# Closing the last expert blocks in order of opening, and combining the last 13 token tiles in three groups

## The chip, the core and the metric

The kernel runs on one core of one Trainium2 chip. The metric is the device time of one execution in microseconds (us). A core has five engines that work side by side and meet at semaphores: TensorE (PE, matrix products; its weight loads are listed as PEld), VectorE (DVE), ScalarE (ACT), GpSimd (POOL) and SyncE (SP). Each takes its instructions in the order of the program, and so does each queue of DMA issues: SP's queue issues the plain transfers here, POOL's the indirect ones (gathers and scatters by a list of row numbers).

## What is computed

The reference is one layer of a graph network on 6250 nodes of 256 features, followed by a mixture of experts. Cut to what matters:

```python
xn = _layernorm(x)
x = x + gnn(xn, edges) + linear_attention(xn)        # 100000 edges
# the experts, on y = _layernorm(x)
gate_logits = y @ gate_w + gate_b                    # 16 experts
topk_vals, topk_idx = jax.lax.top_k(gate_logits, 2)
topk_w = jax.nn.softmax(topk_vals, axis=-1)
h = jax.nn.relu(jnp.einsum('bsh,ehf->bsef', y, w1) + b1)
expert_out = jnp.einsum('bsef,efh->bseh', h, w2) + b2
moe = sum of topk_w * expert_out over the two chosen experts
x = x + _layernorm(y + moe) * gamma + beta
```

## The kernel before

A tile is 128 tokens; there are 49 (`NT`), the last with 106 rows. The kernel works tile by tile through the graph part and the attention. Behind them, when enough tiles have their gate logits, a **phase** (`PHASES`, line 120: tiles 0 to 7, 8 to 11, and so on up to 46 to 48) routes its tiles' tokens to experts. Tokens of one expert are packed into **blocks** of 128 slots, in a buffer in device memory (`w_xslots`). At any time an expert has one open block, which is part full. The phases fill it further, and a full one goes to the end of a queue of blocks to be computed.

- `route` (L771) takes the two best experts of each token, counts, gives each token its slots (`slot_i`), and keeps the state: `s["open"]` is the number of each expert's open block, `s["had"]` whether it has one, `s["queue"]` how many blocks are queued, `s["next"]` the next unused block number, `s["code"]` one number for each place of the queue, which says where the place's block lies and which expert it needs. A small product with the identity (L892) turns `code` into a row, and `listed` (L757) makes the row numbers that SP reads into registers (L968).
- `scatter` (L913) writes the phase's tokens into their slots, by indirect DMAs on POOL (L931).
- `expert` (L964) computes one block j of the queue: SP loads the expert's weights in two pieces (512 KB and 642 KB) and the block's tokens (128 KB), PE transposes (L997) and does both layers (L1007, L1017), ACT the activation (L1013), DVE adds the bias (L1021), and SP stores the block to `w_yslots`. Places for weights: four of each piece.
- `combine` (L1035) finishes two tiles: for each, two gathers from `w_yslots` on POOL (L1047), the normalised token on ACT (L1055), on DVE two weighted additions (L1062), statistics (L315, L316), a normalisation with gamma and beta and the residual (L1070, L1071, L1073), and a store to `out` on SP. There are 14 places for gathered rows.

The number of blocks is fixed at 114 (`USUAL`, L123); places that no tokens fill are computed on a spare row. The phases list 7, 8, ... blocks each; phase 8 lists blocks 63 to 80, phase 9 blocks 81 to 87. The last phase (`flush`) closes all: every expert's open block counts as done, and blocks 88 to 113 are listed in the order of the experts' numbers, an expert's part-full block right behind its full ones.

The order of the work is written by hand. `Weave` (L153) holds pieces of work, each a generator, with the slot at which it goes on; in each slot the pieces that are due issue their instructions, so that every engine's order follows from the slots. Of the later slots: the last phase is routed at 815, block 88 begins at 829 and each next one 4 slots later (block 113 at 929), and a block's store counts as issued 24 slots after its beginning. `combine` of tiles 0 and 1 begins at slot 835, of each next pair 5 slots later. Tiles 36 to 48 are the exception: line 1173 holds them until `block + 24`, slot 953, behind the last block's store.

What a gather waits for is declared by hand too. Every gather would wait for all stores to `w_yslots` issued ahead of it. Phase 8 queues the open blocks that it did not fill as they are (`part`, L818 to L828), so that all tokens of tiles 0 to 35 (`CUT`) lie in blocks 0 to 84 (`FIRST` is 85): their gathers wait for the store of block 84 alone, and not for later ones (L1030 and L1050). The gathers of tiles 36 to 48 wait for all stores.

`usual` (L295) is a flag that the routing multiplies by each of its conditions, such as L894 in the last phase: the queue must be at most 114 blocks long. If one fails, a second pass (L1220 on) computes all 128 possible blocks and combines all tiles again.

Of the kernel before, what the change touches and what calls it, by code (L numbers as in the profile page):

```python
# [23 lines left out]
F32 = mybir.dt.float32  # L24
# [215 lines left out]
def windowed_layer(ctx: ExitStack, tc: tile.TileContext, X, rows3, ident, loc_t, w_t, W, b, gamma, beta, wqT, wkvT, wprojT, bproj,  # L240
# [17 lines left out]
    def one(shape, name, dt=F32):  # L258
        return keep.tile(shape, dt, name=name)
# [468 lines left out]
    s = state("s")  # L728

    def top2(a, b):  # L730

# [22 lines left out]
    def small(name, n=NE, dt=F32):  # L754
        return mp.tile([P, n], dt, name=name, bufs=1)
# [14 lines left out]

    def route(a, b, lo, hi, fresh, part, flush):  # L771

# [126 lines left out]
        if not flush:  # L899
            yield 1  # L900
            if part:
                v.tensor_scalar(old, old, -1.0, 1.0, op0=OP.mult, op1=OP.add)
                v.tensor_tensor(some, some, old, op=OP.mult)
                v.tensor_tensor(left_i, left_i, old, op=OP.mult)
            v.tensor_copy(s["last"], d[:, NE * m:])
            v.tensor_copy(s["fill"], left_i)
            v.tensor_copy(s["had"], some)
            v.scalar_tensor_tensor(first, upto_new, -1.0, s["open"], op0=OP.add, op1=OP.subtract)
            v.tensor_scalar(new, new, 0.0, None, op0=OP.is_gt)
            v.tensor_tensor(first, first, new, op=OP.mult)  # L910
            v.tensor_tensor(s["open"], s["open"], first, op=OP.add)

# [51 lines left out]
    def expert(n, j, homes, bank, gap, apart):  # L964
# [61 lines left out]
        if n is not None:  # L1026
            tc.declare_no_dep(i, group="stores", reason="every block has rows of its own", keep=[before_it])
            tc.add_to_no_dep_group("stores", i)
            stores[j] = i
            if j >= FIRST:  # L1030
                tc.declare_no_dep(i, group="gathers", reason="later blocks hold no token of the first tiles")
                tc.add_to_no_dep_group("late", i)
        homes["y"].give(y_)

    def combine(ts_, homes, pool, last):  # L1035
# [7 lines left out]
        for i, t in enumerate(ts_):  # L1043
            r = rows(t)
            for k in range(2):
                got[i, k] = homes["got"].take()
                g = nc.gpsimd.indirect_dma_start(  # L1047
                    out=got[i, k]()[:r], out_offset=None, in_=yslots,
                    in_offset=IndirectOffsetOnAxis(ap=slot_i[:r, t, k:k + 1], axis=0)).ins
                if t < CUT and FIRST - 1 in stores:  # L1050
                    tc.declare_no_dep(g, group="late", reason="later blocks hold no token of the first tiles")
                    tc.add_manual_dep(g, stores[FIRST - 1].name, mybir.DependencyInfo(mybir.DependencyClass.Sync, mybir.DependencyReason.DATA), reason="the last of their blocks")
                    tc.add_to_no_dep_group("gathers", g)
# [77 lines left out]
    for t in range(4 + RING):  # L1131
        sum_from(t)
    block, ends, scattered = 0, {}, 0
    a = lo = 0
    for n, b in enumerate(PHASES):
        flush = b == NT
        for t0 in range(a, b, 2):
# [11 lines left out]
        weave.add(ready, route(a, b, lo, hi, n == 0, n == AFTER, flush))  # L1149
        if flush or n == AFTER:  # L1150
# [4 lines left out]
        ready += 14 + (2 * (b - a) * slow)  # L1155
        for j in range(lo, hi):
            ends[j] = hi
# [3 lines left out]
            if j == FIRST - 1:  # L1161
                ready_a = block + 24
        lo, a = hi, b
    last = par
    def load_last():
# [4 lines left out]
    weave.add(last_at + RES, load_last())  # L1170
    at = max(ready_a, last_at + RES)
# [566 lines left out]
```

## Time and profile before

| What | us |
|---|---|
| median of 9 runs | 1785.57 |
| lowest and highest of them | 1781.52, 1799.0 |
| the profiled execution's own time | 1784.15 |
| its span, first to last instruction | 1782.4 |
| last routing listed (L769) | 1541.84 |
| first and last gather of `combine` (L1047) | 1556.55, 1746.08 |
| last bias addition of a block (L1021) | 1710.38 |
| last instruction of `combine` on DVE (L1073) | 1768.15 |

How to read the profile: times are us from the span's start. A group or an instruction is named by its line in the kernel, its engine, its operation and the tiles it writes and reads (`out<-in`), with a count (x). In brackets or behind a bar stands the time for which the engine was idle ahead of it, and what ended that idle time, as far as the semaphores show it; "issue" means that nothing in the profile explains it. `Q` is a large buffer whose parts serve as places for weights, tokens and gathered rows. A table by stretches of time gives busy us and the number of instructions of each engine, the granted share of PE's clock, the mean busy share of the 16 DMA engines, and GB/s.

### The profile page before, as it was taken

To read this page: it belongs to the slowest core of one execution; us is meant where nothing else is said; L and a number is where in the kernel's file an instruction comes from. 1 tells how busy PE (TensorE), PEld (TensorE's weight loads), DVE (VectorE), ACT (ScalarE), POOL (GpSimd) and SP (SyncE) were. 2 spreads that over 40 slices of the span, in tenths; PEclk is the share of its full clock that TensorE was granted. 3 is DMA by queue.
4 is the path that set the end of the run, shared out by engine and by line. 5 is a ranking of instruction groups with operands and counts; after the bars stand their busy time and mean duration, and the time that the engine had idled before them with its cause. 6 is when DMAs were issued, how large, how long until landed. Compare 5 with 4: busy or idle time off the path is not lost.

```text
span 1782.4 us, 24227 instructions
## 1 busy us (share of the span) xinstructions
PE 1316.0 (74%) x6930; PEld 1030.4 (58%) x6930; DVE 918.8 (52%) x3262; ACT 505.1 (28%) x1353; POOL 963.6 (54%) x999
## 2 busy tenths in 40 slices
PE   4868888888675877778787786886867888857730
PEld 4635555556444656666566665765756777746620
DVE  8733333357743544544545345354454456359954
ACT  4633333222221212222222122222222233334420
POOL 1046666665576565655656566566665562266341
PEclk9989999977877989888898898889988999889975
DMA  9699432332244656565666565665656776789951
GB/s 290 227 348 371 140 92 86 92 89 84 79 152 148 199 188 219 190 202 193 207 206 205 172 219 186 216 216 184 212 181 199 240 256 219 255 283 391 363 160 53
DMA packets 176557, 357.04 MB, mean 200 GB/s; under 512 B 26643, under 2 KB 115656, under 8 KB 176406
## 3 DMA queue, kind: packets, MB, share of 16 engines
q1 hardware_dynamic: 128458, 226.32, 37.5%
q0 software_dynamic: 47712, 128.17, 22.7%
q8 instruction: 62, 1.02, 0.2%
q10 hardware_dynamic: 236, 0.80, 0.2%
q14 instruction: 89, 0.73, 0.1%
HBM read 280.82 MB, written 74.36 MB: 199 GB/s over the span
## 4 chain that ended last, share of the span: by engine, by line
PE 36%; issue 15%; DVE 13%; another core or an unknown queue 9%; ACT 4%; DMA 3%; POOL 0%; SPq 0%; ACTq 0%; POOLq 0%; DVEq 0%
PE acc L1200 11%; PE yp L1017 9%; PE hp L1007 5%; PE mix L687 3%; PE hp L671 3%; DVE xn L1062 2%; ACT hT L1013 2%; DVE bnst L315 1%; DMA Q<-w_xslots 1%; PE tp L642 1%; PE gl L714 1%; DVE hot L1191 1%; PE xtp L997 1%; DVE xn L1070 1%
## 5 line engine op out<-in xcount | busy, mean ns | idle before, releaser
L1187 POOL DMA_INDIRECT rows<-w_hs,src_t x782 | 759.5, 971 | 586.4 <-PE acc L1200 197.5
L1200 PE MATMUL acc<-rows,hot 128*128 128x256 f32 x1564 | 453.8, 411 | 11.3 <-DMA rows<-w_hs,src_t 8.4
L1200 PEld LDWEIGHTS acc<-rows,hot 128*128 128x128 f32 x1564 | 297.3, 207 | 70.4 <-issue 21.4
L1191 DVE TENSOR_SCALAR hot<-iota_g,loc_t,w_t 128x128 f32<-128x128 f32 x782 | 244.9, 351 | 47.2 <-PE acc L1200 20.5
L1017 PE MATMUL yp<-early,hT 128*128 128x256 f32 x592 | 168.9, 435 | 88.2 <-ACT hT L1013 75.0
L1017 PEld LDWEIGHTS yp<-early,hT 128*128 128x128 f32 x592 | 123.1, 216 | 121.0 <-ACT hT L1013 85.5
L1013 ACT ACTIVATE hT<-hp,early 128x128 f32<-128x128 f32 x296 | 84.4, 369 | 263.2 <-issue 115.3
L1007 PE MATMUL hp<-Q,early 128*128 128x128 f32 x992 | 131.8, 290 | 33.4 <-issue 28.6
L1047 POOL DMA_INDIRECT Q<-w_yslots,slot_i x98 | 99.4, 1014 | 100.8 <-DMA w_yslots<-Q 46.5
L1007 PEld LDWEIGHTS hp<-Q,early 128*128 128x128 f32 x992 | 127.8, 205 | 41.4 <-issue 32.0
L931 POOL DMA_INDIRECT w_xslots<-Q,slot_i x98 | 98.8, 1008 | 85.0 <-ACT hT L1013 56.3
L1021 DVE TENSOR_TENSOR Q<-yp,early 128x256 f32<-128x256 f32 x74 | 31.3, 423 | 192.9 <-PE yp L1017 157.1
L1007 PE MATMUL hp<-Q 128*128 128x128 f32 x832 | 106.4, 281 | 21.6 <-issue 18.0
L1209 DVE SCALAR_TENSOR_TENSOR agg<-acc,dinv,agg 64x256 f32<-64x256 f32 x135 | 65.1, 482 | 102.7 <-remote 55.2
L1007 PEld LDWEIGHTS hp<-Q 128*128 128x128 f32 x832 | 102.8, 196 | 26.1 <-issue 19.9
L1001 ACT COPY Q<-xtp 128x256 f32<-128x256 f32 x114 | 42.1, 369 | 247.5 <-PE xtp L997 129.7
L1017 PE MATMUL yp<-Q,hT 128*128 128x256 f32 x320 | 89.1, 428 | 30.3 <-ACT hT L1013 24.4
L553 PE MATMUL kq<-early,xnT 128*128 128x512 f32 (+1 forms) x196 | 98.9, 628 | 15.1 <-ACT xnT L549 11.1
L559 DVE SCALAR_TENSOR_TENSOR row<-two_a,two_b 128x256 f32<-128x256 f32 (+1 forms) x49 | 20.9, 427 | 154.9 <-ACT two_b L557 94.0
L1017 PEld LDWEIGHTS yp<-Q,hT 128*128 128x128 f32 x320 | 65.2, 214 | 46.8 <-ACT hT L1013 28.3
L321 ACT ACTIVATE sd<-mv,eps_t 128x2 f32<-128x2 f32 (+2 forms) x76 | 22.8, 300 | 205.3 <-DVE mv L316 124.7
L671 PE MATMUL hp<-w_sb,two_a 128*128 128x256 f32 (+1 forms) x196 | 64.8, 460 | 15.6 <-ACT two_a L645 8.5
(272 smaller groups left out, 1779.3 us busy)
## 6 DMA issues: line engine op xcount, KB each, us to landing
early<-in_experts SPq DMA_DIRECT2D x74, 642.0 KB
early<-in_experts SPq DMA_DIRECT2D x62, 512.0 KB
Q<-in_experts SPq DMA_DIRECT2D x52, 512.0 KB
Q<-in_experts SPq DMA_DIRECT2D x40, 642.0 KB
w_xslots<-zero_b SPq DMA_DIRECT2D x16, 1024.0 KB
w_yslots<-zero_b SPq DMA_DIRECT2D x16, 1024.0 KB
Q<-w_xslots SPq DMA_DIRECT2D x114, 128.0 KB
w_yslots<-Q SPq DMA_DIRECT2D x114, 128.0 KB
```

What stands on the lines that cost most here:

```text
L553: nc.tensor.matmul(kq[:r], xnT[:, k, :r], wkq[:, k, :], start=(k == 0), stop=(k == 1))
L671: nc.tensor.matmul(hp[:r0, i, :], agT[:, k, i * P:i * P + r0], w_sb[:, k, :], start=(k == 0), stop=False)
L687: nc.tensor.matmul(mix[:r0, i, :], qT[:, k, i * P:i * P + r0], M[:, k, :], start=(k == 0), stop=False)
L931: i = nc.gpsimd.indirect_dma_start(out=xslots, out_offset=IndirectOffsetOnAxis(ap=slot_i[:r, t, k:k + 1], axis=0), in_=y[:r], in_offset=No ...
L1007: nc.tensor.matmul(hp[:, f, :], w1[:, c, f * P:(f + 1) * P], xT[:, c, :], start=(c == 0), stop=(c == 1))
L1013: act(hT[:, f, :], hp[:, f, :], AF.Relu, bias=b1[:, f:f + 1], scale=1.0)
L1017: nc.tensor.matmul(yp[:, :D], hT[:, f, :], w2[:, f, :], start=(f == 0), stop=(f == FJ - 1))
L1047: g = nc.gpsimd.indirect_dma_start(out=got[i, k]()[:r], out_offset=None, in_=yslots, in_offset=IndirectOffsetOnAxis(ap=slot_i[:r, t, k:k + ...
L1187: nc.gpsimd.indirect_dma_start(out=hrows[c], out_offset=None, in_=hs, in_offset=IndirectOffsetOnAxis(ap=src_t[:, c:c + 1], axis=0))
L1191: v.tensor_scalar(hots[c], iota_g[:, group_of(c) % 2, :], loc_t[:, c:c + 1], w_t[:, c:c + 1], op0=OP.is_equal, op1=OP.mult)
L1200: nc.tensor.matmul(accs[g], hots.pop(c), hrows.pop(c), start=begin, stop=end)
L1209: v.scalar_tensor_tensor(agg(t)[p0:p1], acc[p0:p1, :], dinv[p0:p1, t:t + 1], agg(t)[p0:p1], op0=OP.mult, op1=OP.add)
```

## The change

The last phase is routed like the others: only full blocks are listed, places 88 to 93 of the queue. Then a new piece, `close`, lists the open blocks, in the order in which they were opened: for each expert it counts the open blocks with a smaller number, adds the queue's length, writes those places' `code`, and lists blocks 94 to 113. It runs 1 slot behind the routing, so that its listing falls into slot 834 (block 94 begins at 853).

Because of that order, all tokens of tiles 0 to 39 lie in blocks below 100 if few enough blocks are open, and those of tiles 0 to 45 in blocks below 110. `LIMITS` holds the three groups: tiles up to 35 behind the store of block 84 as before, tiles 36 to 39 behind that of block 99, tiles 40 to 45 behind that of block 109; tiles 46 to 48 go on waiting for all. `combine` begins at the slot of the store that it waits for, or 5 slots behind the pair before: the pairs from 36 on now begin at slots 925, 930, 937, 942, 947, 953 and 958, where they were at 953, 958, ... 983. Three conditions (at most 100, 110 and 114 blocks) are multiplied into `usual`. To compute the first two, the routing of phases 8 and 9 keeps a copy of `s["next"]` (`opened`).

Core of the diff:

```diff
+LIMITS = ((CUT, FIRST), (PHASES[AFTER], 2 * NT + 2), (PHASES[-2], 2 * NT + 12))
...
+    opened = {t: one([P, 1], f"opened{t}") for t, _ in LIMITS[1:]}
...
-    def route(a, b, lo, hi, fresh, part, flush):
+    def route(a, b, lo, hi, fresh, part):
...
         done = whole
-        if flush:
-            done = small("done")
-            v.tensor_copy(done, new)
...
-            listed(row, lo, hi, flush)
-        v.scalar_tensor_tensor(usual, s["queue"][0:1, :], float(hi), usual,
-                               op0=OP.is_le if flush else OP.is_ge, op1=OP.mult)
+            listed(row, lo, hi, False)
+        v.scalar_tensor_tensor(usual, s["queue"][0:1, :], float(hi), usual, op0=OP.is_ge, op1=OP.mult)
...
+        if b in opened:
+            v.tensor_copy(opened[b], s["next"])
+
+    def close(lo, hi):
+
+        earlier = mp.tile([P, NE, NE], F32, name="over", bufs=1)
+        v.tensor_tensor(earlier, s["open"][:, None, :].to_broadcast([P, NE, NE]),
+                        s["open"][:, :, None].to_broadcast([P, NE, NE]), op=OP.is_lt)
+        v.tensor_tensor(earlier, earlier, s["had"][:, None, :].to_broadcast([P, NE, NE]), op=OP.mult)
+        place = small("first")
+        v.tensor_reduce(place, earlier, axis=AX.X, op=OP.add)
+        v.tensor_scalar(place, place, s["queue"], None, op0=OP.add)
+        yield 1
+        v.scalar_tensor_tensor(place, place, iota_p, s["had"], op0=OP.is_equal, op1=OP.mult)
+        d = small("base")
+        v.scalar_tensor_tensor(d, iota_row[:, :NE], 256.0, s["open"], op0=OP.mult, op1=OP.add)
+        v.scalar_tensor_tensor(d, d, iota_p, place, op0=OP.subtract, op1=OP.mult)
+        add = small("add", 1)
+        v.tensor_reduce(add, d, axis=AX.X, op=OP.add)
+        within = small("few", 1)
+        v.tensor_scalar(within, iota_p, s["queue"], None, op0=OP.is_lt)
+        v.scalar_tensor_tensor(s["code"], s["code"], within, add, op0=OP.mult, op1=OP.add)
+        yield 2
+        row = bank("row")
+        nc.tensor.matmul(row[0:1, :P], s["code"], ident, start=True, stop=True)
+        listed(row, lo, hi, True)
+        yield 4
+
+        n = small("add", 1)
+        for t, limit in (*LIMITS[1:], (NT, hi)):
+            if t in opened:
+                v.scalar_tensor_tensor(d, s["open"], opened[t], s["had"], op0=OP.is_lt, op1=OP.mult)
+            v.tensor_reduce(n, d if t in opened else s["had"], axis=AX.X, op=OP.add)
+            v.tensor_tensor(n, n, s["queue"], op=OP.add)
+            v.scalar_tensor_tensor(usual, n[0:1, :], float(limit), usual, op0=OP.is_le, op1=OP.mult)
             yield 1
...
-            if j >= FIRST:
-                tc.declare_no_dep(i, group="gathers", reason="later blocks hold no token of the first tiles")
-                tc.add_to_no_dep_group("late", i)
+            for m, (_, limit) in enumerate(LIMITS):
+                if j >= limit:
+                    tc.declare_no_dep(i, group=f"gathers_{m}", reason="later blocks hold no token of the first tiles")
+                    tc.add_to_no_dep_group(f"late_{m}", i)
...
-                if t < CUT and FIRST - 1 in stores:
...
+                m = next((m for m, (b, _) in enumerate(LIMITS) if t < b), None)
+                if m is not None and LIMITS[m][1] - 1 in stores:
+                    tc.declare_no_dep(g, group=f"late_{m}", reason="later blocks hold no token of the first tiles")
...
-        hi = USUAL if flush else 2 * b - (9 if n < AFTER else -1 if n == AFTER else 4)
+        hi = 2 * b - (9 if n < AFTER else -1 if n == AFTER else 4)
...
+            yield from route(a, b, lo, hi, n == 0, n == AFTER)
+            if flush:
+                yield 1
+                yield from close(hi, USUAL)
...
-        if t0 == CUT:
-            at = max(at, block + 24)
+        at = max(at, stored_at[min(block_of(t0), USUAL) - 1])
         weave.add(at, combine(range(t0, min(NT, t0 + 2)), homes, mp, last))
```

The kernel's `again` pass, which also uses `combine`, keeps its own waits, since it has no entries in `stores`.

More of the change, by code (lines that the diff above doesn't have):

```diff
@@ L892, in route @@
             nc.tensor.matmul(row[0:1, :P], s["code"], ident, start=True, stop=True)
-            listed(row, lo, hi, flush)
-        v.scalar_tensor_tensor(usual, s["queue"][0:1, :], float(hi), usual,
-                               op0=OP.is_le if flush else OP.is_ge, op1=OP.mult)
+            listed(row, lo, hi, False)
+        v.scalar_tensor_tensor(usual, s["queue"][0:1, :], float(hi), usual, op0=OP.is_ge, op1=OP.mult)
         if part:
             v.scalar_tensor_tensor(usual, s["queue"][0:1, :], float(FIRST), usual, op0=OP.is_le, op1=OP.mult)
-        if not flush:
-            yield 1
[L901 to L911, printed above, removed]
@@ new lines, in route @@
+        yield 1
+        if part:
+            v.tensor_scalar(old, old, -1.0, 1.0, op0=OP.mult, op1=OP.add)
+            v.tensor_tensor(some, some, old, op=OP.mult)
+            v.tensor_tensor(left_i, left_i, old, op=OP.mult)
+        v.tensor_copy(s["last"], d[:, NE * m:])
+        v.tensor_copy(s["fill"], left_i)
+        v.tensor_copy(s["had"], some)
+        v.scalar_tensor_tensor(first, upto_new, -1.0, s["open"], op0=OP.add, op1=OP.subtract)
+        v.tensor_scalar(new, new, 0.0, None, op0=OP.is_gt)
@@ new lines, in route @@
+        v.tensor_tensor(first, first, new, op=OP.mult)
+        v.tensor_tensor(s["open"], s["open"], first, op=OP.add)
+        if b in opened:
[30 more added lines that the diff above has]
+            v.scalar_tensor_tensor(usual, n[0:1, :], float(limit), usual, op0=OP.is_le, op1=OP.mult)
+            yield 1
@@ L1049, in combine @@
                     in_offset=IndirectOffsetOnAxis(ap=slot_i[:r, t, k:k + 1], axis=0)).ins
-                if t < CUT and FIRST - 1 in stores:
-                    tc.declare_no_dep(g, group="late", reason="later blocks hold no token of the first tiles")
-                    tc.add_manual_dep(g, stores[FIRST - 1].name, mybir.DependencyInfo(mybir.DependencyClass.Sync, mybir.DependencyReason.DATA), reason="the last of their blocks")
-                    tc.add_to_no_dep_group("gathers", g)
+                m = next((m for m, (b, _) in enumerate(LIMITS) if t < b), None)
+                if m is not None and LIMITS[m][1] - 1 in stores:
+                    tc.declare_no_dep(g, group=f"late_{m}", reason="later blocks hold no token of the first tiles")
+                    tc.add_manual_dep(g, stores[LIMITS[m][1] - 1].name, mybir.DependencyInfo(mybir.DependencyClass.Sync, mybir.DependencyReason.DATA), reason="the last of their blocks")
+                    tc.add_to_no_dep_group(f"gathers_{m}", g)
             y = both[:, i, :]
@@ L1132, in windowed_layer @@
         sum_from(t)
-    block, ends, scattered = 0, {}, 0
+    block, ends, scattered, stored_at = 0, {}, 0, {}
     a = lo = 0
@@ L1146, in windowed_layer, with routed @@
             at += 10
-        hi = USUAL if flush else 2 * b - (9 if n < AFTER else -1 if n == AFTER else 4)
+        hi = 2 * b - (9 if n < AFTER else -1 if n == AFTER else 4)
         ready = max(last_at + RES, scattered - 2)
-        weave.add(ready, route(a, b, lo, hi, n == 0, n == AFTER, flush))
+        def routed(a=a, b=b, lo=lo, hi=hi, n=n, flush=flush):
+            yield from route(a, b, lo, hi, n == 0, n == AFTER)
+            if flush:
+                yield 1
+                yield from close(hi, USUAL)
+        weave.add(ready, routed())
         if flush or n == AFTER:
@@ L1155, in windowed_layer, with block_of @@
         ready += 14 + (2 * (b - a) * slow)
-        for j in range(lo, hi):
-            ends[j] = hi
+        for j in range(lo, USUAL if flush else hi):
+            ends[j] = hi if j < hi else USUAL
             block = max(block + (4 if n > AFTER or block > NCH - 9 else 6 if n == AFTER else 7), ready)
             weave.add(block, expert(n, j, homes, bank, (4, 3) if n < 3 else (5, 4), 5 if block > NCH - 18 else 2))
-            if j == FIRST - 1:
-                ready_a = block + 24
+            stored_at[j] = block + 24
         lo, a = hi, b
+    def block_of(t):
+        return next((limit for b, limit in LIMITS if t < b), USUAL)
     last = par
@@ L1170, in windowed_layer @@
     weave.add(last_at + RES, load_last())
-    at = max(ready_a, last_at + RES)
+    at = last_at + RES
     for t0 in range(0, NT, 2):
-        if t0 == CUT:
-            at = max(at, block + 24)
+        at = max(at, stored_at[min(block_of(t0), USUAL) - 1])
         weave.add(at, combine(range(t0, min(NT, t0 + 2)), homes, mp, last))
```

## The prediction, as put on record

> **What bounds the kernel now.** Only the end of the execution is touched, so I read the page's slices first, then stretches of the end, then the waits in them. In the slices, each digit a fortieth of the span (44.6 us), DVE is full in slices 37 and 38 and POOL nearly idle in the second of them:
>
> ```profile
> DVE  8733333357743544544545345354454456359954
> POOL 1046666665576565655656566566665562266341
> DMA  9699432332244656565666565665656776789951
> ```
>
> The stretches show it finer. The columns are busy us and instruction counts of PE, PEld, DVE, ACT and POOL, then PE's clock, the DMA share and GB/s:
>
> ```profile
> 1613.00:1640.00 27.00, 20.10 (x133) 17.19 (x132) 24.79 (x70) 11.57 (x37) 16.47 (x17) 1.00 1.03 390
> 1640.00:1667.00 27.00, 19.90 (x132) 17.06 (x131) 24.80 (x70) 11.57 (x37) 16.47 (x17) 1.00 1.03 389
> ...
> 1694.00:1713.00 19.00, 13.27 (x85) 11.62 (x84) 7.21 (x20) 7.22 (x23) 0.00 (x0) 1.00 0.62 210
> 1713.00:1735.00 22.00, 0.00 (x0) 0.00 (x0) 14.98 (x43) 3.25 (x9) 16.58 (x17) 0.53 0.41 117
> 1735.00:1749.00 14.00, 0.00 (x0) 0.00 (x0) 5.37 (x14) 0.71 (x3) 9.90 (x10) 0.50 0.35 103
> 1749.00:1769.00 20.00, 0.00 (x0) 0.00 (x0) 17.12 (x48) 2.53 (x7) 0.00 (x0) 0.50 0.14 47
> ```
>
> The reader is to see two things. From 1613 to 1667 every 27 us are alike: DVE does the same 70 instructions, busy for 92%, the rest being the small gaps between dependent ones. These are `combine` of 8 tiles (the stores to `out` at 1610.80, 1637.73 and 1664.73 stand 8 tiles apart) and 5 bias additions (L1021). So DVE sets the pace there, 27.0 / 8 = 3.375 us a tile. Second, from 1694 to 1713 DVE is busy for only 7.2 of 19 us, and from 1713 on no block is left: what runs is `combine` of the last 13 tiles alone. The waits between 1586 and 1700 agree: DVE's only ones are for the square root on ACT, none is for a gather, and POOL is what waits, for places that DVE frees:
>
> ```profile
> POOL Q L1047 <- DVE xn L1062: 27.6, 20, 6.0
> ...
> DVE rs L322 <- issue: 2.2, 6, 0.4
> ...
> DVE rs L322 <- ACT sd L321: 1.1, 3, 0.4
> ```
>
> (in all us, times, longest). And this is the wait that the change takes away, in POOL's order of time, in brackets the idle time:
>
> ```profile
> 1675.05 1.01 POOL L1047 DMA_INDIRECT Q<-w_yslots,slot_i  x1 [1.79 <-DVE row L1073]
> 1713.54 0.94 POOL L1047 DMA_INDIRECT Q<-w_yslots,slot_i  x1 [37.48 <-DMA w_yslots<-Q]
> ```
>
> Tile 35's last gather is at 1675.05, tile 36's first at 1713.54, when the last block's store has landed.
>
> **The end of `combine`.** In the profiled execution tile 35 leaves DVE at 1700.16, and DVE's last instruction ends at 1768.63: 68.5 us. In them DVE waits 14.5 us for PE and for the first gather (1700.16 to 1716.36, less 4 additions of 0.42). From 1735 to 1749 it runs slowly: 5.37 us of work in 14.0, which at a share of 0.92 would have taken 5.8, so 8.2 are lost. I come to that below. In the changed order, tile 36's work stands on DVE between tile 34's and tile 35's, so DVE goes on at the pace of 1613 to 1667: 13 tiles by 3.375 = 43.9 us, to **1744.0** instead of 1768.63. That is 24.6 us less. It holds if four things arrive ahead of DVE:
>
> - Tiles 36 to 39 wait for block 99's store. SP issues it at 1648.41, and POOL comes to these gathers at 1675. No wait.
> - Tiles 40 to 45 wait for block 109's store. On SP it stands behind tile 35's store to `out`: about 1702.3. A store landed 1.70 us behind its issue at 1711.04, POOL began 0.8 us later, and a gather's rows were there 2.83 us after its issue at 1714.79, the second gather being 1.25 behind the first: 1702.3 + 1.7 + 0.8 + 1.25 + 2.83 = 1708.9. DVE comes to tile 40 at 1700.16 + 4 x 3.375 = 1713.7. Cover 5 us. Queued behind a late gather on DVE would be the bias additions of blocks 112 and 113, and behind them the last stores.
> - The additions of blocks 110 to 113 now stand between tiles on DVE, the last at about 1718. PE has had their products since 1701.5 to 1710.4, so DVE finds them done. Their stores wait on SP behind the `out` stores of tiles 36 to 40, which wait for DVE: the last, at 1711.0 before, goes out at about 1720. On ACT, block 113's activations stand behind the square root of tiles 38 and 39, at about 1711; its activations (1.14 us) and PE's product (1.89) then end by about 1715, still ahead of 1718.
> - Tiles 46 to 48 wait for that store: 1720 + 1.7 + 0.8 + 1.25 + 2.83 = 1726.6. DVE is then busy with tiles 42 to 45 and comes to tile 46 at about 1732. Cover 5 us; each us beyond it is a us of the end.
>
> If all cover were gone, the last three tiles would set the end: 1720 + 6.6 + 3 x 3.375 = 1737, still below 1744. So DVE's own work is the bound, not a wait. What follows DVE's end (last stores, the flag's branch, 1768.63 to 1782.4) stays, 13.8 us.
>
> **Added work.** About 36 DVE instructions, most on 16 columns. Like rows are L881 and L887 at 0.19 us each; three of 256 columns are like L1073 at 0.42. That is 7 us at most, 4 of them between the two listings. DVE has room, idle in brackets:
>
> ```profile
> 1544.30 0.42 DVE L1021 TENSOR_TENSOR Q<-yp,Q 128x256 f32<-128x256 f32 x1 [2.23 <-issue]
> 1548.03 0.42 DVE L1021 TENSOR_TENSOR Q<-yp,early 128x256 f32<-128x256 f32 x1 [3.31 <-PE yp L1017]
> ...
> 1555.83 0.42 DVE L1021 TENSOR_TENSOR Q<-yp,Q 128x256 f32<-128x256 f32 x1 [7.37 <-DMA w_yslots<-Q]
> ...
> 1563.85 0.48 DVE L1062 SCALAR_TENSOR_TENSOR xn<-Q,w,xn 128x256 f32<-128x256 f32 x1 [7.58 <-DMA Q<-w_yslots,slot_i]
> ```
>
> That is 20 us of idle time. PE gets one more product (the row, 0.3 us) and waits for its `code`, perhaps to 1549; 1 us is exposed, and PE stands still from 1551.5 to 1555.5 anyway, waiting for the last scatter. If that cover were gone, 4 us. The listing is ready by about 1551, and SP needs block 94's row at about 1590. SP reads registers once more (blocks 94 and 95 by themselves); such a pair took 0.49 + 0.87 us at 1688.5. SP is not the bound there, but every weight load is behind it: between 0 and 1.4, I take 0.7, the middle, as DMA queues are full and DVE waits for nothing.
>
> **Traffic.** 20 gathers and 10 stores of 0.131 MB, 3.93 MB, move into a time in which DMA already runs at 389 GB/s with a share of 1.03. At that rate they take 10.1 us. Half falls behind 1700, where the share was 0.62 and less. DVE waited for no DMA at that rate, and the last weights have 5 us of cover. I take 0, and keep 10.1 as the upper bound.
>
> **Sum.** 1784.15 - 24.6 + 0.7 = 1760.3 for the profiled execution, which lay 1.4 below the median of the runs: **1761.7**.
>
> **The slow pattern.** From 1735 on, DVE's instructions come about one for each gather on POOL, with 0.9 to 1.3 us ahead of one that waits for DVE's own result before it:
>
> ```profile
> 1737.62 0.42 DVE L1073 TENSOR_TENSOR row<-xn,X 128x256 f32<-128x256 f32 x1 [0.91 <-DVE xn L1071]
> ...
> 1739.72 0.48 DVE L1062 SCALAR_TENSOR_TENSOR xn<-Q,w,xn 128x256 f32<-128x256 f32 x1 [1.28 <-DVE xn L1062]
> ```
>
> It begins behind some 16 gathers in unbroken succession (1.25 us apart), and PE shows the like from 1570 to 1585, behind 11 of the first 20. From 1587 to 1675 gathers come 1.7 us apart on average, and no such gap is seen. In the changed order gathers are paced by freed places, with runs of 6 at most. So I take none of it. The Trainium skill (SBUF — State Buffer, Who interferes with whom) speaks against overlapping more of them: a DVE instruction with two inputs in SBUF contends with a GpSimd instruction that reads SBUF, and the one that starts second waits for the whole of the other. By it, the ten tiles moved beside other work gain nothing by the move, since every gather would still hold DVE; the rows from 1613 to 1667 (17 gathers, DVE busy 92%) do not bear that out as a rule for every gather.
>
> **Rivals.**
> 1. *Every gather of the last 13 tiles holds DVE* as between 1735 and 1749: 8.2 us for 10 gathers, 0.82 each, 26 of them 21 us: 1783. For it: those rows. Against it: the steady stretch. For a part of them (6 to 12 gathers in a run) 5 to 10 us: 1767 to 1772.
> 2. *DMA is the bound*: the 10.1 us of traffic delay the last block and all behind it: up to 1772. For it: the share of 1.03. Against: DVE's waits.
> 3. *Slower: a condition fails and everything is computed again.* Counting the reference's own top two experts on the given inputs, the three counts are 99 of at most 100, 106 of 110, 111 of 114. One block more among the oldest sets the flag to the second pass: 128 blocks of 1.41 MB at 389 GB/s are 464 us, and 49 tiles by 3.375 are 165: about 2390. It decides at a single block, and a near tie in a token's choice could only tip it if an expert's count stood at a multiple of 128.
> 4. *The change does not do what it says*, because a gather still waits for all stores: then 1786. POOL's order shows the separate waits, so this is unlikely.
> 5. *A larger gain*: the 13 us that PE lost between 1570 and 1585 shrink, as blocks are listed otherwise: to 1748.
>
> **How the numbers follow.** Forecast with its own errors (1756 to 1767) 0.62; part of rival 1 or 2 (1767 to 1780) 0.20; rival 5 (1748 to 1756) 0.10; no gain (1780 to 1791) 0.03; slower 0.05. 0.3% is 5.4 us, about what a measurement of this kernel can tell from no change. Faster 0.92, same 0.03, slower 0.05. The range 1748 to 1775 holds the forecast, rival 5 and most of the second case, with the bounds of 4 and 10 us.
>
> **What would show it.** The 37 us of POOL's idle time become two waits of a few us or none; stretches of 27 us with 70 DVE instructions go on past 1700; DVE ends near 1744; the last block's store moves from 1711 to about 1720. Wrong would be: DVE waiting for a gather at tile 40 or 46, gaps of 0.9 us between DVE's instructions, PE late with the last four blocks, or a pass after 1782.

## The result and the profile after

| | before | after |
|---|---|---|
| median of the runs, us | 1784.57 (31 runs) | 1754.77 (10 runs) |
| lowest and highest | 1770.66, 1802.30 | 1741.38, 1767.25 |
| ratio of the times | | 0.9846, 95% interval 0.9821 to 0.9871 |
| profiled execution, its span | 1784.15, 1782.4 | 1768.69, 1766.9 |

By the ratio the change takes 27.5 us off, between 23 and 32. The profiled execution of after was a late one: it was already 9 us behind before at the first gather of `combine`, ahead of every `combine` instruction that the change moves, so I compare stretches from that gather on, not clock times. Lines of after: gathers L1083 (before L1047), weighted additions L1099 (L1062), statistics L317 and L318, normalisation L1107, L1108, L1110 (L1070, L1071, L1073), bias addition L1056 (L1021).

| stretch, us | before | after |
|---|---|---|
| first gather to tile 35's first weighted addition | 138.3 | 138.6 |
| from there to DVE's last instruction of `combine` | 73.7 | 49.2 |
| from DVE's end to the span's end | 13.8 | 13.4 |

Nearly all of the gain that the two profiles show from the first gather on, 24.5 of 24.7 us, lies in the second row. The slices of after's page:

```profile
DVE  8733333347754463544534545345355445448996
POOL 1035666566476565565656665665665564055642
```

DVE's busy digits at the end now stand in one piece (8, 9, 9, 6), and POOL's digit in slice 38 is 6, where it was 3. The stretches (busy us and counts of PE, PEld, DVE, ACT, POOL, then PE's clock, DMA share, GB/s):

```profile
1667.00:1694.00 27.00, 20.05 (x130) 17.09 (x130) 24.79 (x70) 11.59 (x38) 16.25 (x17) 1.00 1.02 382
1694.00:1721.00 27.00, 19.86 (x129) 17.11 (x130) 24.52 (x69) 11.68 (x39) 7.03 (x9) 1.00 0.87 303
1721.00:1735.00 14.00, 2.81 (x8) 1.73 (x7) 11.88 (x34) 2.99 (x9) 7.89 (x9) 0.52 0.47 141
1735.00:1749.00 14.00, 0.00 (x0) 0.00 (x0) 12.39 (x35) 1.64 (x5) 5.75 (x5) 0.50 0.30 91
```

The stretches of 27 us with 70 DVE instructions go on to 1721 (70 and 69), and then 14 us hold 34 and 35, which is 66 and 68 for 27 us, nearly the same pace. In before, DVE had 7.2 us of work in 19, and later 5.4 in 14. What became of POOL's wait of 37.48 us, in the order of time on POOL (start, us, in brackets the idle time ahead):

```profile
1684.44 1.00 POOL L1083 DMA_INDIRECT Q<-w_yslots,slot_i  x1 [1.78 <-DVE row L1110]
...
1714.49 0.95 POOL L1083 DMA_INDIRECT Q<-w_yslots,slot_i  x1 [16.95 <-DVE xn L1107]
...
1733.38 0.95 POOL L1083 DMA_INDIRECT Q<-w_yslots,slot_i  x1 [3.98 <-DVE xn L1099]
```

The first line is tile 35's last gather. Tiles 36 to 39 follow it with no wait for block 99. 1714.49 is tile 40 behind block 109's store (SP issues it at 1711.78), 1733.38 is tile 46 behind block 113's (1731.60). The trace names DVE as what came last; both stores wait on SP behind an `out` store that waits for DVE. DVE reached tile 40 at 1723.09 and tile 46 at 1742.59. It waits for no gather.

### The profile page after: what moved, and what is told of

The parts are those of the page before. It is cut to its first block, busy times and chain, and to the rows that moved or that the text cites. A ratio compares the mean times of both kernels' runs of the same rounds, so it can differ in the third digit from the quotient of the medians.

```text
span 1766.9 us, 24266 instructions
## 1 busy us (share of the span) xinstructions
PE 1338.9 (76%) x6932; PEld 1045.9 (59%) x6932; DVE 926.5 (52%) x3298; ACT 505.2 (29%) x1353; POOL 964.1 (55%) x999
## 3 DMA queue, kind: packets, MB, share of 16 engines
q8 instruction: 62, 1.02, 0.2%
## 5 line engine op out<-in xcount | busy, mean ns | idle before, releaser
L1233 DVE TENSOR_SCALAR hot<-iota_g,loc_t,w_t 128x128 f32<-128x128 f32 x782 | 244.8, 351 | 53.7 <-remote 24.7
L1052 PE MATMUL yp<-early,hT 128*128 128x256 f32 x592 | 173.5, 445 | 88.4 <-ACT hT L1048 72.5
L1052 PEld LDWEIGHTS yp<-early,hT 128*128 128x128 f32 x592 | 126.0, 221 | 122.5 <-ACT hT L1048 82.8
L1042 PE MATMUL hp<-Q,early 128*128 128x128 f32 x992 | 132.8, 291 | 33.0 <-ACT Q L1036 16.9
L1083 POOL DMA_INDIRECT Q<-w_yslots,slot_i x98 | 99.4, 1014 | 84.7 <-DVE xn L1099 33.3
L1042 PE MATMUL hp<-Q 128*128 128x128 f32 x832 | 114.5, 294 | 27.2 <-issue 22.5
L1042 PEld LDWEIGHTS hp<-Q 128*128 128x128 f32 x832 | 109.5, 208 | 33.9 <-issue 26.4
L1056 DVE TENSOR_TENSOR Q<-yp,early 128x256 f32<-128x256 f32 x74 | 31.3, 424 | 183.8 <-PE yp L1052 163.1
L555 PE MATMUL kq<-early,xnT 128*128 128x512 f32 (+1 forms) x196 | 101.7, 644 | 13.9 <-ACT xnT L551 13.1
```

What stands on the lines that cost most here:

```text
L555: nc.tensor.matmul(kq[:r], xnT[:, k, :r], wkq[:, k, :], start=(k == 0), stop=(k == 1))
L1042: nc.tensor.matmul(hp[:, f, :], w1[:, c, f * P:(f + 1) * P], xT[:, c, :], start=(c == 0), stop=(c == 1))
L1052: nc.tensor.matmul(yp[:, :D], hT[:, f, :], w2[:, f, :], start=(f == 0), stop=(f == FJ - 1))
L1083: g = nc.gpsimd.indirect_dma_start(out=got[i, k]()[:r], out_offset=None, in_=yslots, in_offset=IndirectOffsetOnAxis(ap=slot_i[:r, t, k:k + ...
L1233: v.tensor_scalar(hots[c], iota_g[:, group_of(c) % 2, :], loc_t[:, c:c + 1], w_t[:, c:c + 1], op0=OP.is_equal, op1=OP.mult)
```

## The experiments

Each session of runs has runs of the kernel before beside it, and every ratio is to those. The sessions fall into two paces, whatever the kernel: before took 1784 us in the first comparison and 1783.5 in one session, and 1505.8, 1505.7 and 1507.6 in three others. One and the same chip showed both paces. I call them the 1784-us and the 1506-us sessions.

In the table, A is the time from the first gather to tile 35's first weighted addition, B from there to DVE's end (profiled execution, us). "Gain" is what the ratio to before makes of that session's median, with its interval.

| kernel | session | A | B | ratio | gain, us |
|---|---|---|---|---|---|
| before, after | 1784 | 138.3, 138.6 | 73.7, 49.2 | 0.9846 | 27 (23 to 32) |
| e0, the change again | 1506 | 125.0 | 48.6 | 0.9879 | 18 (15 to 21) |
| e1, closing alone | 1506 | 125.0 | 65.5 | 0.9990 | 1.5 (-0.5 to 3.5) |
| e2, waits without slots | 1506 | 124.2 | 58.9 | 0.9936 | 10 (7 to 13) |
| e3, two groups | 1506 | 126.0 | 57.3 | 0.9952 | 7 (5 to 10) |
| e4, no residual | 1784 | 147.7 | 46.9 | 0.9892 | 19 (11 to 27) |
| e5, X + beta on POOL | 1784 | 137.7 | 49.4 | 0.9852 | 26 (19 to 33) |
| e6, 8 places | 1784 | 130.3 | 52.3 | 0.9843 | 28 (21 to 35) |
| e7, more traffic | 1784 | 147.1 | 50.9 | 0.9914 | 15 (10 to 21) |
| e8, one DVE op less | 1506 | 120.8 | 43.4 | 0.9795 | 31 (27 to 35) |
| e9, last tiles by PE | 1506 | 124.1 | 47.5 | 0.9862 | 21 (17 to 24) |
| e10, old order, 8 places | 1506 | 124.3 | 65.9 | 0.9996 | 1 (-2 to 3) |
| e11, last stores first | 1506 | 124.5 | 46.2 | 0.9852 | 22 (19 to 26) |

### The change again, and its parts

**e0** is after.py unchanged.

> The changed kernel once more, for a second profile and a second comparison. Theory (DVE sets the pace of the end, and the last 13 tiles now take 24 us less): 25 to 30 us faster than before; first gather of combine to last normalisation on DVE 188 us, where it is 212 before. Rival (part of the 27.5 us that the first comparison gave comes from the stretch ahead of the combine, not from the three groups): first gather to last normalisation shortens by less than 20 us, and the first gather itself comes earlier than 1556 us.

It gained 18 us, not 25 to 30, so the theory missed the size. The rival's figure came, less than 20 us, but its reason is not borne out: against e1 (old order, same session), A is equal and B is 16.9 us shorter, all of the gain. What is missing is in before's own end, as e1 shows.

**e1** closes and lists as the change does, and leaves waits and slots as before:

```diff
-            for m, (_, limit) in enumerate(LIMITS):
+            for m, (_, limit) in enumerate(LIMITS[:1]):
...
-                m = next((m for m, (b, _) in enumerate(LIMITS) if t < b), None)
+                m = next((m for m, (b, _) in enumerate(LIMITS[:1]) if t < b), None)
...
-        return next((limit for b, limit in LIMITS if t < b), USUAL)
+        return next((limit for b, limit in LIMITS[:1] if t < b), USUAL)
```

> The last blocks are closed and listed in the order of their opening as in the change, with its conditions, but the gathers of tiles 36 to 48 wait for all stores and begin at the slots of the kernel before. Theory (the closing is hidden in DVE's idle time and brings nothing by itself): within 3 us of the kernel before, 37 us of idle time on POOL ahead of tile 36 as there. Rival (the new order of the blocks is itself worth something, as SP reads block 94 and later ones in another listing, and block numbers rise with places): 5 us or more faster. Rival (the added listing delays the last blocks): 4 us slower.

The closing by itself is worth nothing and costs nothing. Its last tiles, first POOL's wait, then two stretches:

```profile
1443.47 0.94 POOL L1083 DMA_INDIRECT Q<-w_yslots,slot_i  x1 [37.75 <-DMA w_yslots<-Q]
```

```profile
1460.00:1474.00 14.00, 0.00 (x0) 0.00 (x0) 12.38 (x35) 2.56 (x6) 10.63 (x12) 0.50 0.47 133
1474.00:1490.00 16.00, 0.00 (x0) 0.00 (x0) 14.28 (x40) 1.37 (x4) 3.56 (x3) 0.50 0.25 77
```

The wait of 37 us is there, but DVE works on the 13 tiles at full pace beside POOL's run of gathers: 43.8 us from tile 36's first addition at 1446.28 to the end at 1490.09. In the 1784-us profile of before the same 13 tiles took 52.2 (1716.36 to 1768.58), 8.4 us more. So the old order pays B = 65.5 here and 73.7 there; the new one pays 48.6 and 49.2. So the change gains 16.9 us of idle time in the 1506-us session, and in the 1784-us one about 8 more, where the slow pattern occurs. This last step sets one profile of before beside one of e1; no profile of before was taken at the quicker pace.

**e2** has the change's waits, and only the last of e1's three edits, so that `combine` of tiles 36 to 48 stays behind block 113 in the program's order.

> The change with its three groups of waits for the gathers, but the combine of tiles 36 to 48 stays at the slots of the kernel before, behind block 113 in the order of every engine. POOL's gathers may run early, DVE's work on them may not. Theory (what counts is DVE's order, as DVE sets the end): tile 36's rows are there when the last bias addition is done, so that 5.6 us of waiting for the first gather go, and up to 8 us of the slow stretch, since the gathers are spread: 6 to 14 us faster than before, half the change's gain or less. Rival (the early gathers are the gain, and DVE's order hardly matters): 20 us or more faster.

As the theory had it: 10 us of e0's 18 by the ratios, and 6.6 of 16.9 in B against e1. Tile 36's rows are there, and DVE takes it at 1433.66, right behind the last bias addition (1433.30). What remains is what the slots bring: DVE still idles ahead of the last four additions, 9.9 us in four pieces of 0.9 to 4.3.

**e3** takes the first group away:

```diff
-LIMITS = ((CUT, FIRST), (PHASES[AFTER], 2 * NT + 2), (PHASES[-2], 2 * NT + 12))
+LIMITS = ((CUT, FIRST), (PHASES[-2], 2 * NT + 12))
```

> Tiles 36 to 45 in one group behind the store of block 109, tiles 46 to 48 behind the last: the group of tiles 36 to 39, with its own store, is missing. Theory (DVE must never wait for a gather): DVE is done with tile 35 some 7 us before tile 36's rows can be there, so 7 us of the gain go: 17 to 21 us faster than before. Rival (the last three tiles behind block 113 set the end, so that the first group is hidden): 25 to 30 us faster, as the change. Rival (a run of 12 or 14 gathers one behind the other slows DVE and PE): 10 to 16 us faster.

Gain 7, and 17 to 21 was expected; but that was reckoned from 25 to 28. Against e0 the loss is 11 us by the ratios and 8.6 in B, where 7 was forecast. The waits carry it. DVE's waits behind tile 35 (which ends at 1430.58):

```profile
1431.63 0.42 DVE L1056 TENSOR_TENSOR Q<-yp,Q 128x256 f32<-128x256 f32 x1 [1.05 <-PE xtp L1032]
...
1435.25 0.42 DVE L1056 TENSOR_TENSOR Q<-yp,early 128x256 f32<-128x256 f32 x1 [3.18 <-PE yp L1052]
...
1438.43 0.48 DVE L1099 SCALAR_TENSOR_TENSOR xn<-Q,w,xn 128x256 f32<-128x256 f32 x1 [2.74 <-DMA Q<-w_yslots,slot_i]
1439.94 0.48 DVE L1099 SCALAR_TENSOR_TENSOR xn<-Q,w,xn 128x256 f32<-128x256 f32 x1 [1.02 <-DMA Q<-w_yslots,slot_i]
...
1442.24 0.48 DVE L1099 SCALAR_TENSOR_TENSOR xn<-Q,w,xn 128x256 f32<-128x256 f32 x1 [0.40 <-DMA Q<-w_yslots,slot_i]
```

1.05 + 3.18 + 2.74 + 1.02 + 0.40 = 8.4 us in which DVE has nothing: in the change, tiles 36 to 39 fill them. So the first group is needed too.

### What bounds the combine: DVE or DMA

**e7** adds a load of 128 KB for every tile that nothing reads:

```diff
             sync(out[t * P:t * P + r, :], o[:r])
+            if stores:
+                sync(Q[:, 9 + t % 4, :], experts[t % NE * P:(t % NE + 1) * P, :D])
```

> The changed kernel with one more load of 128 KB for every tile, issued on SP behind the tile's store to out, into a place that nothing reads: 6.4 MB, 16.5 us at 389 GB/s, two thirds of them beside the blocks. Theory (DVE sets the pace and DMA has room): within 4 us of the change. Rival (DMA is the bound beside the blocks): 9 to 13 us slower than the change, with DVE waiting for PE or for gathers between tiles.

The rival's figure: A + B is 10.2 us longer than after's. Three stretches of e7:

```profile
1617.00:1644.00 27.00, 20.30 (x128) 18.09 (x129) 21.72 (x60) 9.91 (x30) 14.28 (x14) 0.94 1.03 367
1644.00:1671.00 27.00, 19.52 (x121) 17.13 (x120) 23.21 (x67) 12.10 (x37) 16.30 (x16) 0.94 1.04 402
1671.00:1698.00 27.00, 19.59 (x119) 16.92 (x119) 24.49 (x68) 11.74 (x36) 12.14 (x12) 0.94 1.05 401
```

DVE falls from 70 instructions in 27 us to 60, 67 and 68, and PE from 130 to between 119 and 128. PE's longest waits from 1600 to 1700 (us, times, longest) are for the blocks' tokens, in e7 and then in after:

```profile
PE xtp L1032 <- DMA Q<-w_xslots: 16.9, 9, 3.5
```

```profile
PE xtp L1032 <- DMA Q<-w_xslots: 10.9, 8, 2.0
```

DVE, for which the rival had waits for PE or for gathers, waited 4.5 us for blocks' stores to land and 1.9 for PE. On SP the waits changed hands in the same 100 us: in after it waits 14.2 us for DVE's rows and 1.6 for loads from the experts' weights to land, in e7 0.4 for rows and 14.3 for such loads. So beside the blocks DMA has little room left. Whether the bytes are the limit or the number of transfers under way is not shown: in the trace SP's transfers use eight semaphores in turn, each waits until the transfer eight issues earlier has landed, and e7's loads take turns as well. The share of 1.03 to 1.05 speaks for the bytes; no run changes the one without the other.

**e4** stores the normalised tile without adding the residual (all 49 tiles).

```diff
-            o = pool.tile([P, D], F32, name="row", bufs=3)
-            v.tensor_add(o[:r], y[:r], X[:r, t, :])
-            sync(out[t * P:t * P + r, :], o[:r])
+            sync(out[t * P:t * P + r, :], y[:r])
```

> The changed kernel without the last addition of each tile on DVE (L1110), in all 49 tiles: the store to out takes the normalised tile, so the output lacks the residual. It takes 0.42 us of DVE's work from every tile, 20 us in all. Theory (DVE sets the pace of the whole combine, also while blocks still run): tile 35 to DVE's end shortens in proportion, 7 instructions of 47 in DVE's share, and the kernel is 14 to 21 us faster than the change, so 32 to 42 us faster than before. Rival (DMA, whose share is 1.03 beside the blocks, sets the pace there, and DVE only behind the last block): only the 13 last tiles gain, 5 to 7 us against the change, 22 to 27 against before.

By the trace, neither (the times alone, 11 to 27 us, do not exclude the rival): A grew by 9 us, and DVE waited 13.1 us for the square root on ACT, once for 5.0. The stores now hold the places of the normalised tokens, which ACT needs for the next ones. It mixes two things and settles nothing, so e8 does it in another way.

**e8** lets the last normalisation write the row that is stored:

```diff
-            v.scalar_tensor_tensor(y[:r], y[:r], rs[:r, i:i + 1], last[:r, 1, :], op0=OP.mult, op1=OP.add)
             o = pool.tile([P, D], F32, name="row", bufs=3)
-            v.tensor_add(o[:r], y[:r], X[:r, t, :])
+            v.scalar_tensor_tensor(o[:r], y[:r], rs[:r, i:i + 1], last[:r, 1, :], op0=OP.mult, op1=OP.add)
```

> The changed kernel without the residual's addition on DVE in all 49 tiles, as in the run before that left it out, but the last normalisation writes the row that the store reads, so that the places of the normalised tokens are not held by the stores. The output lacks the residual. Theory as it now stands (beside the blocks DVE, busy for 92%, and DMA, share 1.03, stand at their limits together; behind the last block DVE alone sets the pace): stretches of 27 us beside the blocks keep some 62 DVE instructions and 130 of PE, and only the last tiles gain, 3 to 7 us against the change, 20 to 34 us faster than before. Rival (DVE alone sets the pace): 14 to 21 us faster than the change, 32 to 48 faster than before, and more than 135 instructions of PE in 27 us.

Between the two. By the ratios it is 13 us faster than e0, by A + B 9.4. Behind tile 35 (B, with 14 tiles by 0.42 = 5.9 us of DVE's work taken away) 5.2 come back: there DVE is the bound. Before it (A, 35 by 0.42 = 14.7) only 4.2 come back:

```profile
1352.00:1379.00 27.00, 19.79 (x131) 17.02 (x130) 22.84 (x65) 12.23 (x39) 17.27 (x18) 1.00 1.04 400
1379.00:1406.00 27.00, 21.98 (x139) 19.65 (x140) 22.37 (x65) 13.14 (x41) 15.75 (x16) 0.94 1.04 402
```

DVE is busy for 83 to 85% and DMA's share is 1.04 at 400 GB/s. The 10.5 us that do not come back are mostly waits of DVE for stores to land, which e0 does not have there (from 1325 to tile 35; us, times, longest):

```profile
DVE row L1109 <- DMA out_dram<-row: 4.9, 5, 1.6
DVE Q L1056 <- DMA w_yslots<-Q: 4.4, 4, 2.6
```

So beside the blocks both are near their limits, DVE at 92% and DMA at 1.02; taking work from DVE alone gave back less than a third of it. There are three places for rows and two for blocks' results, and no run has more, so part of these waits may be due to their number. SP, which issues these stores, waits 23.7 us for weights to land in that stretch, 8.4 in e0. No run takes traffic away.

**e5** forms X plus beta on POOL, so that one of DVE's six instructions of 256 columns for a tile (the expectations of e5 and e9 say seven, which counts the aggregate of 6 columns) goes without leaving anything out:

```diff
+            if stores:
+                nc.gpsimd.tensor_add(Q[:r, 9 + t % 4, :], X[:r, t, :], last[:r, 1, :])
...
+                v.scalar_tensor_tensor(o[:r], y[:r], rs[:r, i:i + 1], Q[:r, 9 + t % 4, :], op0=OP.mult, op1=OP.add)
```

> The changed kernel with X plus beta formed on POOL behind each tile's two gathers, into a place that is free by then, so that DVE's last normalisation writes the output itself and one of its seven instructions of 256 columns per tile goes. The output is the whole one. Theory (DVE is the bound and a POOL instruction beside it costs it little): 32 to 42 us faster than before, as without the residual. Rival (DMA is the bound beside the blocks): 22 to 27 us faster. Rival (POOL's addition and DVE hold each other up): no faster than the change, 15 to 20 us faster than before, and DVE's instructions of 256 columns longer than 0.42 to 0.48 us.

Contrary to that text the output is not the whole one: in the program's order tile t+4's sum overwrites tile t's ahead of its last read, so many tiles add another tile's sum; the work is the same, and only its time is read. The last rival came true, except for its 15 to 20 us against before (26 measured). A + B is 187.1, after's 187.8. Groups of e5 and of after (count, busy us, mean ns):

```profile
L1101 DVE SCALAR_TENSOR_TENSOR xn<-Q,w,xn 128x256 f32<-128x256 f32 x86 | 54.4, 633 | 1.5
...
L1092 POOL TENSOR_TENSOR Q<-X,par 128x256 f32<-128x256 f32 x37 | 30.1, 816 | 17.6 <-DVE row L1112 13.9 <-issue 3.3
```

```profile
L1099 DVE SCALAR_TENSOR_TENSOR xn<-Q,w,xn 128x256 f32<-128x256 f32 x88 | 42.3, 481 | 1.6
```

The weighted additions grew from 481 to 633 ns. In the trace, the 50 that overlap one of POOL's additions took 733 on average and up to 1425, the 38 others 493. In after, the 52 weighted additions that overlap a gather took 483, the 37 others 479: a gather holds DVE for 4 ns at most on average. The Trainium skill (SBUF — State Buffer, Who interferes with whom) says that a DVE instruction with two inputs in SBUF contends with a GpSimd instruction that reads SBUF. These rows bear that out for POOL's arithmetic and not for its gathers.

### The runs of gathers

**e6** is the change with `spare(t) for t in range(41, NT)`, 8 places for gathered rows in place of 14. **e10** is e1 with the same edit.

> The changed kernel with 8 places for gathered rows instead of 14, so that POOL's runs of gathers without a pause are shorter: 8 at the start, where it was 20 and more, and 8 behind the store of block 109, where it was 12. Theory (on a chip that shows PE and DVE starting one instruction per gather in such runs, as the first profiles do, the run costs 10 to 13 us at the start): there 5 to 15 us faster than the change; on a chip that shows no such pattern within 3 us of the change. Rival (the stall at the start is the blocks' wait for their tokens, not the gathers): within 3 us of the change on either. Rival (8 places are too few to cover the way of a gather): slower than the change by 5 us or more, with DVE waiting for gathers.

> The blocks closed as in the change, but the gathers of tiles 36 to 48 wait for all stores, and the combine keeps the slots of the kernel before, with 8 places for gathered rows instead of 14: the order of before with shorter runs of gathers. Theory (on chips with the slow pattern, 8 us of the change's gain are that pattern in the run of 16 gathers behind the last store, and its stall at the start shrinks as well): on such a chip 8 to 16 us faster than before and no gaps of 0.9 us between DVE's instructions near the end; on a chip without the pattern within 3 us of before. Rival (the pattern does not depend on the length of the runs): within 3 us of before on either, the gaps still there.

In the 1784-us session e6 shortens A by 8.2 us. The stall on PE at the start, in after and then in e6:

```profile
1585.81 0.37 PE L1042 MATMUL hp<-Q 128*128 128x128 f32 x1 [2.59 <-issue]
1588.62 0.37 PE L1042 MATMUL hp<-Q 128*128 128x128 f32 x1 [2.44 <-issue]
1590.72 0.37 PE L1042 MATMUL hp<-Q 128*128 128x128 f32 x1 [1.73 <-issue]
1592.82 0.37 PE L1042 MATMUL hp<-Q 128*128 128x128 f32 x1 [1.73 <-issue]
```

```profile
1579.99 0.27 PE L1042 MATMUL hp<-Q 128*128 128x128 f32 x1 [2.64 <-issue]
1582.14 0.37 PE L1042 MATMUL hp<-Q 128*128 128x128 f32 x1 [1.89 <-issue]
```

The first run has 14 gathers without a pause here, not 8, and 20 in after; the run behind block 109 still has 12. So a shorter run came with a shorter stall at the start. But B is 3 us longer, with DVE idle for 3.0 us ahead of the last bias addition (the trace doesn't name for what), and the ratio, 0.9843, is that of the change. Its interval is 7 us to each side, so the times cannot tell the 5 us that are left of it in A + B from nothing. In the 1506-us sessions the pattern is absent. e0 issues its first 42 gathers there without a pause, PE has no gap marked "issue" beside them, and e10 equals e1. A long run of gathers is therefore not enough for it.

### What is next behind DVE

**e9** lets PE sum the last seven tiles (`BY_PE = 42`; ACT makes the two diagonal matrices):

```diff
+            if t >= BY_PE and stores:
+                z = bank("z")[:, :D]
+                nc.tensor.matmul(z[:r], ident[:r, :r], y[:r], start=True, stop=False)
+                for k in range(2):
+                    nc.tensor.matmul(z[:r], Q[:r, 9 + t % 4, k * P:k * P + r], got[i, k]()[:r], start=False, stop=(k == 1))
```

> The changed kernel, but in tiles 42 to 48 PE forms the normalised token plus the two weighted rows (three products into one bank, ACT makes the diagonal matrices of the weights), and DVE reads the sum from there; two of DVE's seven instructions of 256 columns go from each of these seven tiles. The output is the whole one. Theory (behind the last block DVE's own work sets the end): 0.96 us less for each of seven tiles, 5 to 7 us faster than the change in the time from tile 35's first addition to DVE's end, 49 us there. Rival (the gathers of tiles 46 to 48 or the last stores set the end): within 2 us of the change. Rival (PE, whose granted clock is 0.5 once the blocks are done, takes longer than DVE did): slower than the change.

1.2 us in B instead of 5 to 7: the first rival. DVE's and PE's waits for the last tile:

```profile
1462.31 0.43 DVE L318 BATCH_NORM_STATS2 bnst<-z 106x6 f32<-106x256 f32 x1 [4.70 <-PE z L1106]
```

```profile
1459.70 0.65 PE L1106 MATMUL z<-Q 106*106 106x256 f32 x2 [2.56 <-DMA Q<-w_yslots,slot_i]
1461.11 1.16 PE L1106 MATMUL z<-Q 106*106 106x256 f32 x2 [0.76 <-DMA Q<-w_yslots,slot_i]
```

What DVE no longer does it now spends waiting for the gathers of tile 48. POOL issues them at 1453.40 and 1455.27, and PE uses their rows 6.3 and 5.8 us later. By these times the rows of tile 48 would be there in e0 at 1459.3 and 1460.8 (an estimate; it issues the gathers at 1453.04 and 1454.91), and DVE adds them from 1462.59 and 1463.1 on. So the cover of the change is not the 5 us ahead of tile 46 but some 2 us ahead of tile 48's second row, and PE's last products (1.16 us) take part of that.

**e11** is e9 with the last two blocks' stores issued in the slot of their additions:

```diff
-        yield 2
+        if n is None or j < USUAL - 2:
+            yield 2
```

> The run in which PE sums the last seven tiles, and the stores of blocks 112 and 113 issued in the slot of their bias additions instead of two slots later, so that on SP block 113's store stands ahead of the store to out of tile 40. The output is the whole one. In the run without this, 5.8 us lay between block 113's addition and the first gather of tile 46, and DVE then waited 4.7 us for the gathers of tile 48 (through PE). Theory (once DVE's work is smaller, the way from the last addition over the store to the last six gathers sets the end): the addition is followed by tile 46's gather in 2.5 to 3.5 us, and the time from tile 35's first addition to DVE's end goes from 47.5 to 44 to 45 us, so 4 us faster than the change in that stretch. Rival (POOL's six gathers or PE at its lower clock take the time anyway): 46.5 to 48 us, no gain.

From the last addition to tile 46's gather it is 3.9 us (1448.15 to 1452.00) instead of 5.8, but DVE's wait is as long as before, 4.66 us:

```profile
1457.00 1.57 POOL L1085 DMA_INDIRECT Q<-w_yslots,slot_i  x1 [0.30 <-DVE mv L319]
...
1466.54 0.43 DVE L318 BATCH_NORM_STATS2 bnst<-z 106x6 f32<-106x256 f32 x1 [4.66 <-PE z L1107]
```

POOL now issues its last 18 gathers without a pause, 1436.27 to 1458.88, and tile 48's come last: its first rows are used 6.3 us after their gather, as in e9. So POOL's run of gathers and the way of tile 48's rows take the time. B is 46.2, 1.3 us less than e9's, between the theory's 44 to 45 and the rival's 46.5 to 48. Its ratio, 0.9852, lies below e0's 0.9879, but the intervals overlap: 2.5 us less in B is what the traces show, and the times alone do not part the two.

## Why the prediction was right, step by step

The forecast was 1761.7 and the change gave 1754.77: 23.9 us less were forecast, 27.5 measured (23 to 32). For the points in time I take 9.42 off the late profile of after, which sets tile 35's first weighted addition to the same time in both.

- **DVE's pace gives the end.** Right: DVE's end at 1744.1 (1744.0 forecast), tile 40 at 1713.7 (1713.7), tile 46 at 1733.2 (1732); B is 24.5 us shorter, forecast 24.6. (DVE's end before is 1768.58 in the trace, not 1768.63, and POOL's digit in slice 38 was 3, which is not "nearly idle".) That the size fits is in part luck of the pace: 8.2 of the 24.6 us are the slow stretch, and in the 1506-us session, which does not have it, the same change gained 18.
- **The waits.** Tile 40's first gather at 1705.1 (1704.8), so a cover of 5 us. Block 113's store issued at 1722.2 (1720), tile 46's rows at about 1728.0 (1726.6), a cover of 5 us. Last bias addition at 1717.8 (1718). The working named the last three tiles as the next bound, and e9 bears that out. But it priced tile 46 alone, with 2.83 us from a gather to its rows; tile 48's took about 6 in e9 and e11, so the bound lies some 2 us below DVE's end, not 7 (1737 against 1744).
- **The added work.** Hidden, as forecast, though DVE's work grew by 7.7 us (926.5 against 918.8 on the pages; 7 at most was forecast): e1 is within its interval of before, and the 0.7 us for the register pair cannot be told from nothing.
- **"So DVE sets the pace there."** Only half right. It is what failed in the working. Beside the blocks the way through SP and DMA is as full as DVE (e7: 10.2 us for 16.5 us of traffic; e8: 4.2 us back for 14.7 of work). The trace had the share of 1.03, and I took the absence of waits for DMA on DVE as proof of room; the waits were on PE, for tokens (13.8 us of them between 1586 and 1700 in before). Behind the last block DVE is the bound (e8: 5.2 of 5.9), with the small cover that e9 found. There the change works, so the sum came out.
- **Traffic at nothing.** Right in size (A is 138.34 and 138.55, 0.2 us), but not for the reason given: by e7, 3.93 MB more beside the blocks would have cost some 6 us (an estimate: 10.2 by 3.93 / 6.4). Most of the moved traffic fell behind 1694, where the share is 0.87 (303 GB/s) and less.
- **The slow pattern.** The 8.2 us are real where it occurs and are part of the gain (8.4 us in the 13 tiles, before against e1). The forecast of runs of 6 gathers at most was wrong: 12 stand without a pause from 1714 to 1728. The pattern stayed away even so, though not entirely: DVE shows gaps of 0.25 us at 1730 behind them, and none of 0.9. That runs of gathers make it is half the truth, since the 1506-us sessions have the runs and not the pattern.
- **The rivals.** Every gather holding DVE did not occur: 483 against 479 ns. The condition did not fail, no second pass follows. The larger gain of rival 5 did not come: the stall at the start is as long as before (A).

What stays open is what makes the two paces, and with them the pattern. In the 1784-us profile of before the chain that ended last is "issue" for 15% of the span and another core or an unknown queue for 9%; in e1's, 5% and none. After's chain covers only 16% of its span and cannot tell. PE's mean granted clock differs as well: 0.88 to 0.89 in before's 17 runs beside e4 to e7, 0.93 to 0.94 beside e0 to e3 and e8 to e11; whether that is a cause or a consequence is not shown. No run here sets the pace.

## What to carry to other kernels

When an engine is idle behind a wait for everything, look for an order in which parts are finished early, and move the consumers in the program's order too: the waits alone brought 6.6 of 16.9 us (e2 against e1), and one group fewer lost 8.6 us (e3). "No waits on this engine" does not show that DMA has room; look at who waits for tokens or weights, or add a load that nothing reads. Before taking work from the busiest engine, look at how much cover each later wait has, the last one too: here 5 us at tile 46 but some 2 at tile 48, and e9 ran into that after 1.2.

## What the hardware showed that I had not expected

- The same kernel took 1784 or 1506 us by the session, on one chip too, and the difference lies ahead of the combine above all (first gather at 1556.6 and 1299.6 us, before and e1).
- POOL's addition of 128x256 beside DVE: 816 ns on POOL, and weighted additions of up to 1425 ns on DVE, where 481 is usual. Moving DVE's addition there gained nothing (e5).
- The gathers of tile 48, with 106 rows, took 1.56 us each on POOL against 0.95 for 128 rows, and in e11 the first one's rows were used 6.3 us after its issue (1457.00 to 1463.31), where tile 36's first in before were used after 2.8 (1713.54 to 1716.36).
